# A fp32 attention and gated-scan block on Trainium2: low fp16 halves moved from GpSimd to VectorE, and the first chunk's split of x put later

## The chip, the core and the metric

The kernel runs on one NeuronCore of one Trainium2 chip. The core's engines run their own instruction queues in order: TensorE (PE; its weight loads are shown apart, as PEld), VectorE (DVE), ScalarE (ACT), GpSimd (POOL) and SyncE (SP), which here only issues DMAs. The metric is the device time of one execution in microseconds (us): the median of several runs, lower is better.

## The reference

The input x is 2 sequences of 2048 tokens with 256 features, in fp32. A layer of hierarchical linear attention comes first: 16 heads, 64 features for queries and keys, 16 for values. The weight of key s for query t is the score, times a decay that grows with the distance, times a level weight chosen by the position of s against t.

```python
decay = jnp.exp(jnp.where(tri[None, :, :, None], diff, NEG))
lam_ts = jnp.take_along_axis(Lam[:, :, :, None, :], levels[None, :, None, :, None], axis=-1)[..., 0]
scores = jnp.einsum('bthd,bshd->bhts', Q, K) * S ** (-0.5)
Wmat = scores * jnp.transpose(decay, (0, 3, 1, 2)) * jnp.transpose(lam_ts, (0, 2, 1, 3))
Y = jnp.einsum('bhts,bshd->bthd', Wmat, V).reshape(Bb, Tt, H * HD)
o = Y @ Wout.T + x
```

o is normalized, x is added, and the sum is normalized again. A gated recurrence follows. It scans over the first axis, so it has two steps, with the 2048 tokens as its batch: `c = f * c + i * g` with sigmoid and tanh gates, then `h = tanh(x @ wo.T + c_final @ uo.T + bo)`. A last residual sum and normalization give the output.

## The kernel before, in words

**Chunks.** The tokens are cut into 16 chunks of 128 (`NC`), and each chunk holds both sequences. For each chunk c the program records `load_x`, `project`, `keys`, `attend` and `finish` (the loop at the end of `body`). Within a chunk the attention is computed directly. Earlier chunks come in through states `Nst`, kept like the digits of a binary counter.

**Split numbers.** TensorE is fed fp16. An fp32 operand is split into a high half (rounded to fp16) and a low half (the fp32 value less the high half, as fp16), and a product takes three matmuls: high by high, low by high, high by low (`terms`). The halves that matter here:

- `xth`, `xtl`: x of the chunk with features on the partitions, 128x512 (`load_x`, lines 617 to 627). For chunk 0 ACT makes xth and DVE xtl. For the chunks 1 to 15 DVE casts xth and POOL subtracts to get xtl. They feed the projections `pv` (values, level weights, step sizes) and `pqk` (queries and keys).
- `xnh`, `xnl`: x with tokens on the partitions (lines 628 to 633), for the chunks 0 to 14. ACT makes xnh and POOL xnl, from the staging tile `xn`, which has one buffer.
- `wvh`, `wvl`: the decayed values `wv` (lines 751 to 756), for the chunks 0 to 14. POOL makes wv from the values and a decay `E`, ACT makes wvh, POOL wvl. The matmul `pu` multiplies xn by wv; its result becomes `Uh`, `Ul`, and through the key weights (`pS`) the chunk's state.

**Engines around them.** ACT evicts most PSUM tiles as high halves (`F` of pqk, `YT`, `Uh`, `tr_x`), takes the exponentials (`DL` of the matmul `arg`, `E`) and the gates' tanh (`tg`). DVE makes the low halves that come out of PSUM (`L`, `Ul`, `YTl`), multiplies scores by weights (`DL<-sc,DL`), and has the normalizations (`st`, `mv`, `o`, `x`, `hh`). POOL has small work on the log weights `LL` (rows of levels, decay and leaf terms), the inverse roots `rs`, `Yi`, `Yl`, the state sums and residual sums. In `project`, ACT writes logarithms into LL (two evictions from m), then cumulative sums (the eviction from `pc`). DVE splits LL into `RP`, PE transposes it, ACT evicts it as `RT`, and DMAs spread it (`cg`, `scr`, `st`, `R`) for the matmul `arg`.

**The order.** Nothing is issued while `body` runs. A `Recorder` keeps every engine call as an operation; PE calls that accumulate into one tile are joined. `depend` finds what each must wait for. `order` (lines 382 to 516) then makes one list of all operations: a list scheduler that walks through a modelled timeline and takes, for each engine, the ready operation with the earliest due time. The due times are read from the string `PLAN`, two characters per operation; the costs come from `cost`; tile buffers (`BUFS`) and PSUM banks (`BANKS`) are handed out in the same walk. `issue` (lines 518 to 529) emits the list, so that each engine's queue has its operations in that order, all of them from line 529, which is why the profile shows that line nearly everywhere. SP's queue has the DMAs in the list's order too. During the first chunk it also carries the weights: `wo` and `fw` come in 256 KB pieces through two staging buffers, ACT and DVE split them (`wo_h`, `wo_l`, `fw_h`, `fw_l`), and a piece can only be loaded when the buffer is free.

Of the kernel before, what the change touches and what calls it, by code (L numbers as in the profile page):

```python
# [110 lines left out]
    'Yh': 1, 'Yl': 1, 'acc0': 1, 'tq': 1, 'acc1': 3, 'acc2': 5, 'st69': 2, 'mv9': 10, 'rs9': 5,  # L111
}
BANKS = {'y': 8, 'z': 5, 'x': 8, 'a': 7, 's': 8, 'p': 6, 't': 5,}
MERGE, WARM, TABLE, MODE = 0.6, 0.37, 1.28, 0.1


# [36 lines left out]
class View:  # L153
# [20 lines left out]
    def real(self):  # L174
        ap = self.tile.real()
        for name, a, k in self.chain:
            ap = getattr(ap, name)(*a, **k)
        return ap
# [63 lines left out]
class Recorder:  # L242
# [139 lines left out]
    def order(self, code):  # L382
# [26 lines left out]
        for key, q in queue.items():  # L409
            free[key] = BANKS[key[1]] if key[0] == "bank" else BUFS.get(key[1], 1)  # L410
            for k, t in enumerate(q):
# [106 lines left out]
    def issue(self, plan):  # L518
        real = lambda v: v.real() if isinstance(v, View) else v
        with self.tc.manual_schedule():  # L520
            table = AF.Ln
            for i in plan:
                f = self.ops[i].fn
                if f == AF.Ln and table != f:
                    self.tc.nc.scalar.preload_act_table_set("natural_log_exp_and_others")
                if f in (AF.Ln, AF.Tanh):
                    table = f
                for eng, meth, a, k in self.ops[i].calls:
                    getattr(eng.real, meth)(*[real(x) for x in a], **{q: real(x) for q, x in k.items()})  # L529


def body(tc, A, out, nblk=NC):
    nc = tc.nc
    with ExitStack() as es:
# [2 lines left out]
        ps = es.enter_context(tc.tile_pool(name="ps", bufs=1, space=PSUM))  # L537
        dr = es.enter_context(tc.tile_pool(name="dr", bufs=1, space=DRAM))
        rec = Recorder(tc)
        V, G, ACT, PE, SP = (Engine(rec, n, e) for n, e in (  # L540
            ("DVE", nc.vector), ("POOL", nc.gpsimd), ("ACT", nc.scalar), ("PE", nc.tensor), ("SP", nc.sync)))

# [536 lines left out]
            finish(c)  # L1079
        rec.depend()  # L1080
        plan = rec.order(PLAN)
        rec.issue(plan)


# [43 lines left out]
```

## Time and profile before

| | |
|---|---|
| median of 3 runs | 613.0 us (612.38 to 614.44) |
| the profiled execution, whole | 613.06 us |
| its span, first to last instruction | 611.3 us |
| mean granted TensorE clock | 0.988 |
| DMA | 38.59 MB, 63 GB/s mean; 1 queue of SP |
| chain that ended last | PE 50%, DVE 17%, POOL 16%, ACT 8% of the span |
| largest groups of DVE | `L<-pqk,F` 85.6 us x128, `DL<-sc,DL` 84.4 us x128 |
| largest groups of POOL | `rs<-rs,mhalf` 33.8 us x45, `Yi<-Yi,tq` 24.9 us x32 |

How to read the profile: a group line has the line of code, the engine, the operation, `out<-in` by the program's names, the shape, and the count; behind the first bar the busy time in us and the mean of one in ns; behind the second the time that the engine stood idle just before them, and who ended that wait. A timeline line begins with the start and the duration in us from the span's start; idle time before it stands in brackets. A matmul's end is modelled, and matmuls overlap in the pipeline, so PE's busy time is not time at its peak. The span and the whole time differ by 1.76 us, which lie outside the first and last instruction.

### The profile page before, as it was taken

To read this page: it belongs to the slowest core of one execution; us is meant where nothing else is said; L and a number is where in the kernel's file an instruction comes from. 1 tells how busy PE (TensorE), PEld (TensorE's weight loads), DVE (VectorE), ACT (ScalarE), POOL (GpSimd) and SP (SyncE) were. 2 spreads that over 40 slices of the span, in tenths; PEclk is the share of its full clock that TensorE was granted. 3 is DMA by queue.
4 is the path that set the end of the run, shared out by engine and by line. 5 is a ranking of instruction groups with operands and counts; after the bars stand their busy time and mean duration, and the time that the engine had idled before them with its cause. 6 is when DMAs were issued, how large, how long until landed. Compare 5 with 4: busy or idle time off the path is not lost.

```text
span 611.3 us, 24225 instructions
## 1 busy us (share of the span) xinstructions
PE 578.4 (95%) x10362; PEld 499.2 (82%) x10362; DVE 495.4 (81%) x1166; ACT 395.5 (65%) x946; POOL 333.6 (55%) x677
## 2 busy tenths in 40 slices
PE   6878999999999999999999999999999999999895
PEld 3666889988898878898888988889888889888794
DVE  5678886969787986979789698896969888897985
ACT  5467687646595877568674677576577774556442
POOL 3465737334764859356593374765487663335332
PEclk9997999999999999999999999999999999999898
DMA  7753221301032103302214012130403112101101
GB/s 235 194 145 112 61 61 38 111 4 53 14 116 62 54 23 87 99 3 66 65 31 118 3 54 61 54 79 3 129 2 101 31 35 64 36 2 27 54 2 35
DMA packets 54155, 38.59 MB, mean 63 GB/s; under 512 B 16616, under 2 KB 52200, under 8 KB 54016
## 3 DMA queue, kind: packets, MB, share of 16 engines
q1 hardware_dynamic: 54048, 37.05, 21.2%
q8 instruction: 81, 1.33, 0.9%
q14 instruction: 26, 0.21, 0.1%
HBM read 29.70 MB, written 7.34 MB: 61 GB/s over the span
## 4 chain that ended last, share of the span: by engine, by line
PE 50%; DVE 17%; POOL 16%; ACT 8%; issue 4%; DMA 3%; SPq 1%; POOLq 0%; ACTq 0%; DVEq 0%
PE pqk L529 14%; PE gt L529 11%; PE sc L529 5%; PE pi L529 4%; POOL rs L529 3%; DVE st L529 2%; PE pv L529 2%; PE ph L529 2%; PE pin L529 2%; PE arg L529 2%; DMA xn<-x 2%; POOL LL L529 2%; DVE o L529 2%; PE po L529 2%; DVE DL L529 2%
## 5 line engine op out<-in xcount | busy, mean ns | idle before, releaser
L529 ACT ACTIVATE F<-pqk 128x512 f16<-128x512 f32 x128 | 75.8, 598 | 36.7 <-PE pqk L529 35.8
L529 DVE SCALAR_TENSOR_TENSOR L<-pqk,F 128x512 f16<-128x512 f32 x128 | 85.6, 679 | 12.0 <-ACT F L529 11.4
L529 PEld LDWEIGHTS <-fw_h 128*128 128x128 f16 x1176 | 91.6, 98 | 2.0 <-issue 0.2
L529 DVE SCALAR_TENSOR_TENSOR DL<-sc,DL 128x512 f32<-128x512 f32 x128 | 84.4, 680 | 7.8 <-PE sc L529 6.3
L529 PE MATMUL gt<-tr_x,fw_h 128*128 128x128 f16 x768 | 83.3, 220 | 0.9 <-DVE tr_x L529 0.8
L529 ACT ACTIVATE DL<-arg 128x512 f32<-128x512 f32 x128 | 72.4, 607 | 11.0 <-PE arg L529 10.8
L529 PEld LDWEIGHTS <-wk_h 128*128 128x128 f16 x992 | 71.0, 98 | 9.0 <-issue 2.3
L529 ACT ACTIVATE tg<-gt,gb 128x128 f32<-128x128 f32 x192 | 56.1, 372 | 34.2 <-PE gt L529 31.5
L529 PEld LDWEIGHTS <-F 64*128 64x128 f16 x2048 | 63.0, 95 | 13.1 <-issue 8.9
L529 PE MATMUL pqk<-xth,wq_h 128*128 128x256 f16 x256 | 70.2, 274 | 2.2 <-DVE Ul L529 1.9
L529 PE MATMUL gt<-tr_x,fw_l 128*128 128x128 f16 x384 | 70.3, 219 | 0.0
L529 PE MATMUL pqk<-xth,wk_h 128*128 128x256 f16 x256 | 70.2, 274 | 0.0
L529 PE MATMUL pqk<-xth,wq_l 128*128 128x256 f16 x256 | 70.1, 274 | 0.0
L529 PE MATMUL pqk<-xtl,wk_h 128*128 128x256 f16 x256 | 70.1, 274 | 0.0
L529 PE MATMUL pqk<-xtl,wq_h 128*128 128x256 f16 x256 | 70.0, 274 | 0.0
L529 PE MATMUL pqk<-xth,wk_l 128*128 128x256 f16 x256 | 70.0, 273 | 0.0
L529 PEld LDWEIGHTS <-fw_l 128*128 128x128 f16 x588 | 57.4, 98 | 1.7 <-issue 1.0
L529 PEld LDWEIGHTS <-wq_h 128*128 128x128 f16 x512 | 47.1, 98 | 10.8 <-issue 3.7
L529 PE MATMUL sc<-F 64*128 64x128 f16 x512 | 48.6, 222 | 2.1 <-ACT F L529 1.6
L529 PEld LDWEIGHTS <-wk_l 128*128 128x128 f16 x496 | 46.3, 98 | 4.3 <-issue 1.0
L529 PE MATMUL arg<-R,st 96*128 96x64 f16 x1024 | 45.3, 193 | 3.6 <-ACT DL L529 2.1
L529 PE MATMUL sc<-F,L 64*128 64x128 f16 x512 | 47.6, 221 | 0.5 <-DVE L L529 0.5
(185 smaller groups left out, 1842.2 us busy)
## 6 DMA issues: line engine op xcount, KB each, us to landing
st<-cg SPq DMA_DIRECT2D x16, 512.0 KB
xt<-xT SPq DMA_DIRECT2D x16, 256.0 KB
xc<-x SPq DMA_DIRECT2D x16, 256.0 KB
xn<-x SPq DMA_DIRECT2D x15, 256.0 KB
out<-hh SPq DMA_DIRECT2D x15, 256.0 KB
scr<-RT SPq DMA_DIRECT2D x16, 160.0 KB
R<-scr SPq DMA_DIRECT2D x32, 80.0 KB
stg_fw<-fw SPq DMA_DIRECT2D x8, 256.0 KB
```

What stands on the lines that cost most here:

```text
L529: getattr(eng.real, meth)(*[real(x) for x in a], **{q: real(x) for q, x in k.items()})
```

## The change

It does two things after the plan is made; `PLAN`, `BUFS`, costs and the recorded operations are as they were, so `order` returns the same list as before.

First, at issue, every operation whose result is xtl, xnl or wvl, and which was recorded for POOL, is emitted on DVE instead, at its place in the list. Second, three operations are moved within the list: ACT's first xnh goes behind the last operation of chunk 0 that ACT does into LL (the eviction of pc), the first xnl behind the last operation of chunk 0 that POOL does into E, and the load of xn for chunk 1 behind that xnl, since xn has one buffer.

```diff
+LOW = ("POOL:xtl", "POOL:xnl", "POOL:wvl")
...
                 for eng, meth, a, k in self.ops[i].calls:
+                    if self.ops[i].kind.split("@")[0] in LOW:
+                        eng = self.dve
                     getattr(eng.real, meth)(*[real(x) for x in a], **{q: real(x) for q, x in k.items()})
...
         rec = Recorder(tc)
+        rec.dve = Engine(rec, "DVE", nc.vector)
...
         plan = rec.order(PLAN)
+
+        seen = lambda kind: [k for k, i in enumerate(plan) if rec.ops[i].kind == kind]
+        for kind, other in (("ACT:xnh@0", "ACT:LL@0"), ("POOL:xnl@0", "POOL:E@0"), ("DMA:xn", "POOL:xnl@0")):
+            a, b = seen(kind)[0], seen(other)[-1]
+            if a < b:
+                plan.insert(b, plan.pop(a))
         rec.issue(plan)
```

## The prediction

> **What bounds the kernel now.** I read, in this order: the busy shares and slices, a table by stretches, the groups by form, and the timelines of ACT, DVE and POOL at the places of the change. The page's shares and slices first (tenths of each fortieth of the span; PEclk is the granted TensorE clock):
>
> ```profile
> PE 578.4 (95%) x10362; PEld 499.2 (82%) x10362; DVE 495.4 (81%) x1166; ACT 395.5 (65%) x946; POOL 333.6 (55%) x677
> ...
> PE   6878999999999999999999999999999999999895
> ...
> PEclk9997999999999999999999999999999999999898
> ```
>
> PE is full from slice 5 on; DVE comes second. The table by stretches (stretch, its length, then busy us of PE, PEld, DVE, ACT, POOL, the granted clock, DMA):
>
> ```profile
> 20.00:60.00 40.00, 31.29 (x400) 24.46 (x398) 28.39 (x51) 25.57 (x60) 23.50 (x52) 0.92 0.52 149
> 60.00:150.00 90.00, 89.47 (x1758) 78.13 (x1757) 74.17 (x176) 60.89 (x145) 44.80 (x88) 1.00 0.20 57
> 150.00:300.00 150.00, 147.37 (x2708) 127.72 (x2706) 125.49 (x300) 104.58 (x255) 91.55 (x189) 1.00 0.21 60
> 300.00:450.00 150.00, 146.10 (x2621) 127.21 (x2618) 123.32 (x284) 101.83 (x246) 87.95 (x184) 1.00 0.19 54
> 450.00:570.00 120.00, 116.80 (x2187) 101.81 (x2180) 101.02 (x254) 73.94 (x178) 67.24 (x128) 1.00 0.15 42
> ```
>
> From 20 to 60 us PE is idle 40.00 − 31.29 = 8.7 us, at a clock below 1. From 60 to 570 us it is idle only 510 − 499.7 = 10.3 us. There DVE is busy 424.0 of 510 us, so idle 86. A gain can come from the first 60 us; a loss comes where DVE hands PE its next operand late. DVE has spare time on the mean; whether it has it where the new instructions stand decides.
>
> **The change, part by part.**
>
> *What moves.* I compared the two programs engine by engine. PE's order is the same. POOL loses 45 instructions and DVE gains them (15 each of xtl, xnl, wvl), at the place of the common order where they stood. On ACT the first xnh goes from ahead of the two LL evictions of m to just behind the LL eviction of pc. On SP one 256 KB load of fw goes ahead of the xn load of chunk 1. The rows that price the 45:
>
> ```profile
> L529 POOL TENSOR_TENSOR xtl<-xt,xth 128x512 f16<-128x512 f32 x15 | 18.3, 1223 | 11.3 <-DVE xth L529 11.3
> L529 POOL TENSOR_TENSOR xnl<-xn,xnh 128x512 f16<-128x512 f32 x15 | 18.1, 1207 | 30.3 <-ACT xnh L529 30.3
> L529 POOL TENSOR_TENSOR wvl<-wv,wvh 128x512 f16<-128x512 f32 x15 | 18.1, 1205 | 3.0 <-ACT wvh L529 3.0
> ```
> ```profile
> L529 DVE TENSOR_TENSOR xtl<-xt,xth 128x512 f16<-128x512 f32 x1 | 0.7, 693 | 1.8 <-ACT xth L529 1.8
> ```
>
> The last row is the same operation on DVE, seen once: 0.69 us. In a row of like instructions DVE starts the next 0.60 to 0.61 us later (two L of 0.68 take 1.29 in its timeline), so each new one costs the queue behind it 0.61 us: 45 × 0.61 = 27.5 us of DVE, against 54.5 us taken off POOL.
>
> *What comes back.* A large POOL instruction holds some DVE instructions up:
>
> ```profile
> 35.76 1.54 DVE L529 SCALAR_TENSOR_TENSOR m<-z 128x416 f32<-128x416 f32 x1
> ```
> ```profile
> 35.70 1.15 POOL L529 TENSOR_TENSOR xtl<-xt,xth 128x512 f16<-128x512 f32 x1
> ```
>
> m<-z takes 0.58 us elsewhere; here it lasts to the end of POOL's xtl and 0.4 beyond. Over the trace I summed, for DVE instructions that lay beside one of the 45, the time above the tenth percentile of their form: 8.6 us in 15 places. So DVE's net gain in load is 27.5 − 8.6 = 18.9 us. [...]
>
> *First chunk (20 to 57 us).* ACT now:
>
> ```profile
> 25.01 0.63 ACT L529 ACTIVATE xnh<-xn 128x512 f16<-128x512 f32 x1 [4.66 <-DMA xn<-x]
> 25.54 0.32 ACT L529 ACTIVATE LL<-m 128x160 f32<-128x160 f32 x1
> ...
> 27.27 0.64 ACT L529 ACTIVATE wo_h<-stg_wo 128x512 f16<-128x512 f32 x1
> ...
> 28.26 0.65 ACT L529 ACTIVATE fw_h<-stg_fw 128x512 f16<-128x512 f32 x1
> 28.78 0.24 ACT L529 ACTIVATE LL<-pc 128x64 f32<-128x64 f32 x1
> ```
>
> ACT stands 4.66 us before xn, whose last part lands at 24.98 by the trace's completions. Behind it wait two LL, three F, VZ and all the weight splits. PE loses 1.62 us at 24.8 and 0.49 at 26.6 to those F and to their L: 2.1 us that go. But not 4.66 us: ACT then reaches wo_h, whose load lands only at 26.92, so wo_h starts 27.27 − 26.95 = 0.3 us earlier than now, LL<-pc ends at 28.7 instead of 29.02, and behind it now stands xnh (0.52). What is late next: POOL's E no longer waits behind its leaf work (30.92 now); it goes to 28.8. wv, wvh and RT follow; RT's end, 34.61 now, goes to about 32.4 (E<-E 29.7, two Ne to 30.15, wv 31.2, wvh 31.9, RT 32.4): 2.2 us. On DVE the new xnl stands ahead of RP and waits for xnh, to 29.3, then 0.69: RP starts at 30.1 instead of 31.00, a gain of 0.9 there. wvl, now on DVE, ends at 33.2 instead of 35.24, and pu with it: 2.0 us. The second chunk's xnl waits 0.34 us on DVE for its xnh, with u<-m,u, an Ul and L behind it; with the four new instructions between 35 and 54 us that is 0.34 + 4 × 0.61 = 2.8 us, and the held-up m (twice), fw_l and u give 0.96 + 0.96 + 0.97 + 0.37 = 3.3 back, so I set it at nothing. The moved xn load now waits for xnl (30.1 instead of 26.9), with a load of fw behind it at 30.5 instead of 29.9; xn is not read before about 36, so nothing. I take **−2.0 us** for this part; the ends are 0 (the L and DMA waits around 40 to 50 us eat it) and −5.4. The lower end has 3.4 us for the clock: it is granted at half from 53.9 to 60.75 us, with PE busy throughout, so 6.83 × 0.5 = 3.4 us hang on PE's idle time just before (0.67, 0.28 and 1.04 us at 49.4 to 52.2, for L and for ACT's DL).
>
> *After 60 us.* The semaphores tell which DVE instruction each PE instruction waits for. For every new place I followed them from the DVE instruction behind it and took the least time that lies free before some PE instruction would start late. Delay is 0.61 per new instruction, plus its wait, less DVE's idle time there, less what collisions give back. In us:
>
> 61.6 xnl: 0.59 wait + 0.61, free 0.07: loss 1.1. 102.8 to 115.5, three: 1.83, free 0.91: 0.9. 175 to 179, two: 1.22, free 0.37: 0.85. 210 to 216, three: 1.83 − 0.75 given back, free 0.03: 1.05. 286 to 288, three: 1.83 − 0.34, free 0.35: 1.1. 318 to 329, four: 2.44 − 1.60, free 0.67: 0.2. 393 to 405, three: 1.83 − 0.77, 0.36 idle: 0.7. 429 to 432, three: 1.83 − 0.31, free 0.05: 1.5. 463 to 471, three: 1.83 − 0.71, free 0.12: 1.0. The other 13 together 0.8, eight of them nothing (76, 90, 188, 230, 241, 362, 485, 494: free 0.9 to 3.3, or as much idle or given back).
>
> Sum 9.2 us; with the 2.7 above the upper end is 11.9. The lower end is 0: DVE's 86 us of idle time, and 1.9 us that PE waits for POOL (gp at 206 and 354, Yl at 411 and 456) which POOL, relieved of a sixth of its work, may give back. The places were priced one by one, and PE, once late, is late for the next one too, so they add up to less than 9.2. I take the middle, **+6.0 us**.
>
> *Sum.* 611.3 − 2.0 + 6.0 = 615.3 us of span. The profiled execution took 613.06 us, 1.76 us around its span; it is level with the median of 613.0. So **617.0 us**.
>
> **Rivals.** (a) *Hidden*, 612: the new instructions fall into DVE's idle time and only the first chunk's −2.0 and about +1 remain. For it: 86 us of idle. Against it: from 102 to 125 and from 319 to 339 us DVE's idle time adds up to under 0.7 us, against 1.8 and 2.4 us of new instructions. (b) *Faster*, 609: the half-clock stretch at 53.9 us goes. PE's idle time of 2.0 us at 49.4 to 52.2 us would have to shrink, which it does if ACT has wvh and DL out earlier; 613.06 − 2.0 − 3.4 + 1.4 = 609.1. It decides the sign from a loss under 5.4 us after 60 us. [...] (c) *DVE the bound*, 630: each of the 45 is charged in full, 613.06 + 18.9 − 2.0; for it, DVE at 81% would be at (495.4 + 18.9)/611 = 84%; against it, 97 us of idle would remain on the mean. (d) *Level*, 613 to 614.8: first chunk and rest cancel.
>
> **Numbers.** A measurement of this kernel tells 0.3% from no change, 1.8 us. Forecast (615 to 622) 0.47, (a) 0.20, half of it below 611.2, (b) 0.12, of which 0.10 below 611.2, (c) 0.11, (d) 0.10. Faster 0.10 + 0.10 = 0.20; same 0.10 + 0.02 + 0.10 = 0.22; slower 0.58. The range takes in (b), at 609.0, and reaches to 613.06 + 11.9 = 625.0, which leaves out (c) and a little else. The forecast's own range is 615 to 622.
>
> **What would show it.** First chunk: ACT's wait of 4.66 us before xnh gone, its idle time now before wo_h, RT ending near 32.4 us, PE idle in 20:60 at 6.7 instead of 8.7. After: PE's idle in 60:570 up from 10.3 to about 16, ended by DVE (Ul, L, DL, tr_x); DVE busy near 514; m<-z back at 0.58. It would be wrong if PE's idle after 60 us stays near 10, or if xnl is found waiting for xnh on DVE for more than the 0.3 to 0.6 us worked out here.

## The result, and the profile after

The changed kernel takes 619.85 us (median of 4 runs, 619.0 to 620.99), the kernel before 612.95 us beside it: ratio 1.0109, 95% interval 1.0096 to 1.0122, so it is slower by 1.1%. The profiled execution took 620.22 us, its span is 618.4 us (before 611.3), the mean clock 0.988 as before.

The page after, the lines that answer to those of before:

```profile
PE 581.0 (94%) x10362; PEld 499.9 (81%) x10362; DVE 513.0 (83%) x1211; ACT 395.8 (64%) x946; POOL 285.8 (46%) x632
...
PE   5797999999999999999999999999999999999895
...
PEclk9997999999999999999999999999999999999899
```

DVE has its 45 instructions more (1211 against 1166) and is 17.6 us busier; POOL is 47.8 us less busy. The table by stretches, same columns as before:

```profile
20.00:60.00 40.00, 32.73 (x436) 25.11 (x434) 31.74 (x60) 25.87 (x60) 16.21 (x45) 0.88 0.53 152
60.00:150.00 90.00, 88.32 (x1726) 77.18 (x1719) 75.02 (x180) 59.86 (x145) 37.37 (x81) 1.00 0.19 56
150.00:300.00 150.00, 145.20 (x2636) 124.92 (x2634) 129.80 (x306) 101.70 (x249) 74.70 (x172) 1.00 0.22 60
300.00:450.00 150.00, 144.79 (x2546) 125.61 (x2544) 126.80 (x298) 100.14 (x238) 74.70 (x162) 1.00 0.20 54
450.00:570.00 120.00, 118.44 (x2185) 103.39 (x2182) 100.11 (x244) 77.86 (x188) 60.35 (x128) 1.00 0.13 37
```

PE's idle time is 7.3 us from 20 to 60 (before 8.7) and 510 − 496.75 = 13.25 us from 60 to 570 (before 10.3). That is not the whole loss: for the matmuls that stand from 60 to 570 us in the trace of before, PE's busy time grows from 499.7 to 502.9 us, though they are the same matmuls, so part of the loss is counted as busy. A better measure is the start of each matmul. Both kernels have the same 10362 in the same order, so the traces can be laid side by side, matmul by matmul. PE is ahead of before by 1.02 us at 43 us and by 1.48 at 57 us; it is behind by 0.47 at 150, 4.2 at 300, 6.0 at 450 and 6.9 at 560 us. This "lag" is used from here on; it compares one execution with one.

The 1.48 at 57 us is not all gain. In both traces the clock is at half rate for 6.83 us, from 53.92 us before and from 54.00 after. The lead is 1.02 us up to that stretch, and since the same work reaches the stretch 1 us earlier, more of it runs ahead of the stretch at the full rate; at the other end this goes back, and the lead is 1.10 us where PE meets the first wait after it:

```profile
62.12 1.08 PE L532 MATMUL pi<-DL,VZ 128*32 128x128 f32 x32 [0.82 <-DVE DL L532]
```

So the first chunk gave 1.0 us, and what follows took 7.9.

The moved subtractions, by form, on DVE:

```profile
L532 DVE TENSOR_TENSOR xtl<-xt,xth 128x512 f16<-128x512 f32 x16 | 11.8, 738 | 1.9 <-ACT xth L532 1.9
L532 DVE TENSOR_TENSOR wvl<-wv,wvh 128x512 f16<-128x512 f32 x15 | 10.8, 723 | 0.7 <-ACT wvh L532 0.7
...
L532 DVE TENSOR_TENSOR xnl<-xn,xnh 128x512 f16<-128x512 f32 x15 | 10.3, 687 | 0.7 <-ACT xnh L532 0.7
```

They take 0.69 to 0.74 us. The xnl wait 0.7 us in all and the wvl 0.7 us; the 1.9 us before xtl belong to chunk 0, whose xtl was on DVE before too. The m that was held up takes 0.59 us again:

```profile
35.04 0.59 DVE L532 SCALAR_TENSOR_TENSOR m<-z 128x416 f32<-128x416 f32 x1
```

**One place in detail.** How the time is lost shows where three of the 45 stand close together. DVE's timeline before (start, duration), then after:

```profile
428.69 0.73 DVE L529 TENSOR_SCALAR hh<-hh,mv,rs 128x256 f32<-128x256 f32 x2
429.35 0.68 DVE L529 SCALAR_TENSOR_TENSOR L<-pqk,F 128x512 f16<-128x512 f32 x1
...
431.38 0.67 DVE L529 SCALAR_TENSOR_TENSOR DL<-sc,DL 128x512 f32<-128x512 f32 x1
...
432.31 0.67 DVE L529 TENSOR_TENSOR Ul<-pu,Uh 128x512 f16<-128x512 f32 x1
```
```profile
433.24 0.74 DVE L532 TENSOR_SCALAR hh<-hh,mv,rs 128x256 f32<-128x256 f32 x2
433.89 0.69 DVE L532 TENSOR_TENSOR xtl<-xt,xth 128x512 f16<-128x512 f32 x1
434.49 0.69 DVE L532 SCALAR_TENSOR_TENSOR L<-pqk,F 128x512 f16<-128x512 f32 x1
...
436.22 0.68 DVE L532 TENSOR_TENSOR xnl<-xn,xnh 128x512 f16<-128x512 f32 x1
436.81 0.69 DVE L532 SCALAR_TENSOR_TENSOR DL<-sc,DL 128x512 f32<-128x512 f32 x1
...
437.74 0.68 DVE L532 TENSOR_TENSOR wvl<-wv,wvh 128x512 f16<-128x512 f32 x1
438.33 0.69 DVE L532 TENSOR_TENSOR Ul<-pu,Uh 128x512 f16<-128x512 f32 x1
```

DVE comes here 4.55 us late (hh). L is 5.14 us later than before, DL 5.43, Ul 6.02: DVE has no pause, so each new instruction adds its 0.6 us, less 0.3 that the two `o<-o,rs,xc` take without POOL's subtraction beside them (0.88 us instead of 1.18). PE, also 4.5 us late when it comes here, stands twice and leaves 6.0 us late:

```profile
437.55 0.27 PE L532 MATMUL pqk<-xth,wq_h 128*128 128x256 f16 x1 [0.32 <-DVE DL L532]
439.08 0.40 PE L532 MATMUL arg<-R,st 96*128 96x64 f16 x8 [0.71 <-DVE Ul L532]
```

The waits shown are single short ones (the longest after 60 us is 1.05 us); no line of the page holds the loss. Nor does POOL's relief come through: its wait for DVE's m ahead of g is 42.0 us instead of 16.0, for DVE's z 48.4 instead of 32.7. And POOL's own work grew longer: 54.5 us of instructions went, its busy time fell by 47.8 only.

**The first chunk.** ACT no longer waits for xn; it waits for wo's load instead:

```profile
26.73 0.63 ACT L532 ACTIVATE wo_h<-stg_wo 128x512 f16<-128x512 f32 x1 [3.62 <-DMA stg_wo<-wo]
27.26 0.58 ACT L532 ACTIVATE F<-pqk 128x512 f16<-128x512 f32 x1
27.74 0.62 ACT L532 ACTIVATE fw_h<-stg_fw 128x512 f16<-128x512 f32 x1
28.26 0.21 ACT L532 ACTIVATE LL<-pc 128x64 f32<-128x64 f32 x1
```

LL<-pc stands behind it, RP on DVE behind LL, xnl and two weight splits. PE's two stops of 1.62 and 0.49 us (for F and L) are gone and it runs 2.9 us ahead, to stand 3.46 us in one piece. The first two rows are from the kernel after, the third from the kernel before:

```profile
30.79 0.71 PE L532 MATMUL pt<-idh,RP 128*128 128x128 f16 x5 [3.46 <-DVE RP L532]
...
41.79 0.36 PE L532 MATMUL pv<-wv_h,xth 128*128 128x464 f16 x1 [0.63 <-DVE L L532]
```
```profile
42.82 0.36 PE L529 MATMUL pv<-wv_h,xth 128*128 128x464 f16 x1 [0.80 <-DVE L L529]
```

The last two rows are the same matmul, the last common point: PE waits there for an L of DVE before and after, and leaves 1.02 us earlier.

### The profile page after: what moved, and what is told of

It reads as the page before. It is cut to its first block, busy times and chain, and to the rows that moved or that the text cites. A ratio compares the mean times of both kernels' runs of the same rounds, so it can differ in the third digit from the quotient of the medians.

```text
span 618.4 us, 24210 instructions
## 1 busy us (share of the span) xinstructions
PE 581.0 (94%) x10362; PEld 499.9 (81%) x10362; DVE 513.0 (83%) x1211; ACT 395.8 (64%) x946; POOL 285.8 (46%) x632
## 4 chain that ended last, share of the span: by engine, by line
PE 44%; DVE 27%; POOL 12%; ACT 7%; issue 5%; DMA 4%; SPq 1%; POOLq 0%; ACTq 0%; DVEq 0%
PE gt L532 12%; PE pqk L532 8%; PE sc L532 4%; DVE L L532 4%; PE pi L532 4%; POOL rs L532 3%; DVE st L532 3%; DVE DL L532 3%; PE pv L532 3%; DVE o L532 2%; PE ph L532 2%; PE pin L532 2%; DMA xn<-x 2%; PE po L532 2%; PE arg L532 2%
## 5 line engine op out<-in xcount | busy, mean ns | idle before, releaser
L532 ACT ACTIVATE tg<-gt,gb 128x128 f32<-128x128 f32 x192 | 56.1, 371 | 35.4 <-PE gt L532 32.7
L532 PEld LDWEIGHTS <-L 64*128 64x128 f16 x1024 | 47.0, 95 | 1.7 <-issue 1.1
```

## The experiments

Times are medians; the ratio is to the kernel before on the same chip, with its 95% interval. The last four columns are PE's lag against before, in us (negative: ahead), at that time of the trace of before; each is of one execution, and the executions of one kernel lie 1 to 4.4 us apart. Lags at 57 us lie inside the half-rate stretch that every kernel has there and are distorted by it. The two kernels with copies leave the low halves concerned out, so they are no versions to use.

| kernel | us | ratio | 43 | 57 | 150 | 560 |
|---|---|---|---|---|---|---|
| the change | 619.85 | 1.0109 [1.0096, 1.0122] | −1.0 | −1.5 | +0.5 | +6.9 |
| moves only | 611.63 | 0.9986 [0.9971, 1.0000] | −1.0 | −0.9 | 0.0 | −0.3 |
| halves only | 620.47 | 1.0131 [1.0114, 1.0148] | −1.2 | −0.7 | +1.2 | +7.8 |
| moves, 16 free halves | 611.19 | 0.9975 [0.9965, 0.9985] | −1.2 | −1.2 | −1.9 | −1.9 |
| moves, 29 costly halves | 620.23 | 1.0135 [1.0118, 1.0152] | −0.7 | −1.2 | +1.5 | +8.1 |
| both engines subtract | 645.54 | 1.0537 [1.0507, 1.0567] | +1.8 | +2.1 | +6.7 | +32.5 |
| copies in place of halves | 609.12 | 0.9946 [0.9924, 0.9967] | −2.8 | −3.4 | −2.9 | −4.9 |
| change, RP ahead | 620.72 | 1.0136 [1.0097, 1.0174] | −1.1 | −0.7 | +2.6 | +9.2 |
| 16 free, RP ahead | 610.88 | 0.9970 [0.9953, 0.9987] | −1.2 | −1.7 | −2.2 | −2.0 |
| and 2 fw splits late | 611.83 | 0.9963 [0.9942, 0.9984] | −1.7 | −1.9 | −2.6 | −2.1 |
| and 4 fw splits late | 616.23 | 1.0033 [1.0018, 1.0048] | −4.2 | +2.6 | +2.3 | +2.9 |
| change, PE kept busy | 619.93 | 1.0087 [1.0062, 1.0113] | −1.7 | −1.5 | +0.5 | +7.0 |
| change, 5 early copies | 619.14 | 1.0072 [1.0049, 1.0095] | −2.3 | −2.0 | 0.0 | +6.5 |

**Where the loss comes from.** Theory A: each added instruction makes DVE's operands late by its own length, at the places without free time, and these add. The rivals: the moves of the first chunk cost it (B), or DVE's load as such does, wherever the instructions stand (C). The first four kernels split the change in two ways: by its two parts, and by the places that the prediction had priced at nothing or nearly so (16) and the rest (29).

```diff
-LOW = ("POOL:xtl", "POOL:xnl", "POOL:wvl")
+LOW = ()
```

> The three moves in the list alone; all low halves stay on POOL. Theory A (late operands: an instruction put on DVE costs where PE's next operand from DVE has less free time than the 0.61 us it takes, and these losses add up): nothing changes after 60 us, the first chunk gains 0.5 to 2 us, so 611.0 to 612.5 us. Rival B (the moves in the list are what costs): 615 us or more, PE 3 us or more later than before at 60 us.

For the second, the five lines after `rec.order(PLAN)` that move three operations are left out.

> The 45 low halves on DVE, the list's order as before. Theory A: the loss of 8 us after 60 us stays, the first chunk gains nothing (DVE now waits for xn as ACT does), so 620 to 623 us. Rival B (the moves in the list cost): 613 us or less.

For the third and fourth, LOW lists which of the 15 of each kind go to DVE:

```diff
+LOW = {"xtl": (1, 2, 3, 11), "xnl": (1, 2, 4, 8, 15), "wvl": (1, 2, 3, 6, 8, 11, 15)}
...
-                    if self.ops[i].kind.split("@")[0] in LOW:
+                    if nth[low] in LOW.get(low, ()):
```

> As the change, but of the 45 only the 16 that the prediction priced at about nothing are on DVE (seven in the first 60 us, nine later), 29 stay on POOL. Theory A: level with the moves alone to within 1 us, 611 to 613 us. Rival C (DVE's added load counts wherever it stands): 16/45 of the 8 us on top of the moves alone, 614.5 us.

> As the change, but only the other 29 on DVE, in the places that the prediction priced (and four that it priced at 0.1 to 0.3 us). Theory A: nearly all of the loss after 60 us, 7 to 8 us above the moves alone, 618.5 to 620.5 us. Rival C (load wherever it stands): 29/45 of 8 us, 5.2 us above the moves alone, 617 us.

The moves alone are level (611.63). The halves alone have the whole loss (620.47), and the gain of the first chunk as well (1.2 us at 43 us), which the expectation had at nothing. The 16 free ones cost nothing: 611.19 against 611.63 for the moves alone, with intervals that overlap, so a gain is not shown. The 29 have the whole loss again, 8.1 us at 560 us. B and C fall. The parts add: at 560 us, 16 free and 29 costly stand 1.6 under and 8.4 above the moves alone; −0.3 − 1.6 + 8.4 = 6.5, and the change has 6.9.

**DVE's own time, or its consumers?** In one kernel POOL keeps its 45 and DVE does each a second time into a spare tile; in another DVE has a copy of the high half at each place instead of the subtraction, so that the low half is left out.

```diff
-                        eng = self.dve
+                        self.dve.real.tensor_tensor(self.spare, real(a[1]), real(a[2]), a[3])
```

> The 45 subtractions stay on GpSimd, as before the change, and the vector engine does each of them a second time, into a tile that nobody reads, at the place where the changed kernel has it; the moves of the first chunk are in. (Nothing of the computation is left out; the second copies are extra work.) Theory A (the vector engine's own later operations come late, by the 0.6 to 0.75 us that each added instruction occupies, at places where little is free): the same loss as the change, 619 to 623 us, more than the change rather than less, because GpSimd now works beside it. Rival (the time is lost because TensorE, the consumer, waits for halves that now come late out of the vector engine's queue): consumers get their halves from GpSimd as before, so 611 to 613 us.

```diff
-                        eng = self.dve
+                        self.dve.real.tensor_copy(real(a[0]), real(a[2]))
+                        continue
```

> The changed kernel, with each of the 45 subtractions on the vector engine replaced by a copy of the high half (fp16 to fp16), which I estimate at 0.2 to 0.4 us from the vector engine's CAST 128x512 (0.42 us) against 0.69 to 0.74; the low halves are then wrong, this part of the computation is left out. Theory A (loss is the time that the added instruction occupies at places with little free time, beyond the first part that is free): most of the loss goes, 612 to 615 us. Rival (the loss is a matter of order and waits: the vector engine's queue stands until ScalarE has made the high half, whatever the length of the instruction): 618 to 620 us.

Both decide for A, and both missed in size. The useless second subtraction costs 32.5 us, nearly five times the change, although nobody reads it. Its rows, by form:

```profile
L531 DVE TENSOR_TENSOR spare<-xt,xth 128x512 f16<-128x512 f32 x15 | 18.2, 1214 | 0.0
L531 DVE TENSOR_TENSOR spare<-xn,xnh 128x512 f16<-128x512 f32 x15 | 15.1, 1004 | 0.7 <-ACT xnh L532 0.7
L531 DVE TENSOR_TENSOR spare<-wv,wvh 128x512 f16<-128x512 f32 x15 | 15.0, 1000 | 1.7 <-ACT wvh L532 1.7
```

Both engines become ready at the same moment and read the same two tiles: DVE takes 1.00 to 1.21 us instead of 0.69, POOL 1.29 to 1.42 instead of 1.21 to 1.22. That is 48 us of DVE instead of 31. POOL's halves come later too, but that is not what PE waits for. Over the matmuls that stand between 60 and 570 us in the trace of before, PE's waits that end on DVE sum to 5.4 us before, 10.6 in the change, 26.2 here and 4.0 with the copies; those that end on POOL stay at 1.9, 1.7, 2.0 and 1.7. The copies (median 0.28 us, mean 0.28 to 0.34) take nearly the same places and the loss is gone, with 4.9 us gained at 560 us. So what counts at these places is the length of the new instruction, not that one stands there. Where the 4.9 us come from was not separated.

**Why the first chunk gave less.** First theory (part of Theory A in the next two expectations, B' later): the one standstill of 3.46 us ahead of RP, and the half-rate window that follows it, are what is missing. Two kernels put the splits of wo, of the first fw and of xn, and gb, behind RP, once in the changed kernel, once with the 16 free halves:

```diff
+        a, b = seen("ACT:wo_h@0")[0], seen("DVE:RP@0")[-1]
+        names = ("ACT:wo_h@0", "DVE:gb@0", "DVE:wo_l@0", "ACT:fw_h@0", "DVE:fw_l@0", "DMA:stg_fw@0",
+                 "ACT:xnh@0", "POOL:xnl@0")
+        late = [i for i in plan[a:b] if rec.ops[i].kind in names]
+        plan[a:b + 1] = [i for i in plan[a:b + 1] if i not in late] + late
         rec.issue(plan)
```

> The changed kernel, with one more move in the first chunk: the operations that split the loads of wo and of the first fw, gb and the first chunk's x (two of them wait for loads that land at 26.2 and 26.7 us) are placed behind the second RP, so that the LL <- pc of ScalarE and the two RP of the vector engine don't queue behind them. Theory A (of the gain in the first chunk, the part that is missing sits in the one standstill of TensorE ahead of RP, 3.46 us from 27.3 to 30.8, and in the half-rate window that follows it, some 1.7 us): the standstill shrinks to below 1 us, and 2.5 to 5 us come off, 615 to 617.5 us. Rival (the next wait, the transposed RT with its way through the scratch in DRAM or the weights' splits, takes its place): 619 to 620.5 us.

> The same move on top of the version with the 16 halves that cost nothing on the vector engine and the other 29 on GpSimd (611.2 us, where the standstill ahead of RP is 3.81 us with no half-rate window behind it). Theory A: 2 to 3.5 us off, 607.5 to 609.5 us, faster than both kernels. Rival (another wait takes its place): 610.5 to 611.5 us.

The standstill goes, and nothing is gained: 620.72 and 610.88. PE stands elsewhere, and goes on at 41.7 us, where it waits for the L, as in the changed kernel. PE's rows in the changed kernel with RP ahead, then the row of ACT that is behind the second:

```profile
30.61 0.27 PE L532 MATMUL pqk<-xth,wq_h 128*128 128x256 f16 x1 [2.03 <-DVE L L532]
37.42 0.27 PE L532 MATMUL pqk<-xth,wq_h 128*128 128x256 f16 x1 [2.72 <-DVE Ul L532]
```
```profile
34.61 0.63 ACT L532 ACTIVATE fw_h<-stg_fw 128x512 f16<-128x512 f32 x1 [3.60 <-DMA stg_fw<-fw]
```

So two theories were left. C (the letter is used anew from here on): DVE's row of work up to that L sets the end (in the changed kernel the timeline shows 0.3 us of idle time between 27.4 and 42.3 us). D: the landing of fw's pieces does. Two kernels put the next two fw splits behind Ul, or those behind the third L after it and the following two behind five DL:

```diff
+        def late(names, a, b):
+            moved = [i for i in plan[a:b] if rec.ops[i].kind in names]
+            plan[a:b + 1] = [i for i in plan[a:b + 1] if i not in moved] + moved
...
+        fw = ("ACT:fw_h@0", "DVE:fw_l@0", "DMA:stg_fw@0")
+        late(fw, seen("ACT:fw_h@0")[1], seen("DVE:Ul@0")[-1])
```

> The version with 16 halves on the vector engine and the move ahead of RP (610.9 us), in which the split of the second and third load of fw (fw_h on ScalarE, fw_l on the vector engine) is also placed behind the first chunk's second Ul. Theory C (the end of the first chunk is set by the vector engine, which has hardly a pause from 27.4 us to the L that TensorE awaits at 41.7; a step that only changes the order ahead of that L gives nothing): TensorE is at 42.8 us where it was, 610 to 611.5 us. Theory D (it is set by the landing of the fw load, for which ScalarE stood 3.6 us ahead of 34.6 us once RP came early): the 2 us that TensorE stood ahead of Ul go, 607.5 to 609.5 us.

```diff
-        late(fw, seen("ACT:fw_h@0")[1], seen("DVE:Ul@0")[-1])
+        late(fw, seen("ACT:fw_h@0")[1], [k for k in seen("DVE:L") if k > seen("DVE:Ul@0")[-1]][2])
+        late(fw, seen("ACT:fw_h@0")[3], seen("ACT:DL@0")[4])
```

> As the run before, but the splits of the second and third load of fw are placed behind the third L that follows Ul, and the next two behind the first five DL of ScalarE. Theory C: two fw_l (0.69 us each) leave the vector engine's row ahead of the L at 41.7, so TensorE is 1.0 to 1.4 us ahead from 42.8 us on, 608.5 to 610 us, unless pg, which needs the fifth fw_l, then waits (it would by 1 us or more: 610 to 611). Theory D: no further gain over the run before.

With the first of them PE's wait for the first Ul goes (2.0 us with 16 free halves and RP ahead), and its wait for L doubles from 0.6 to 1.2 us. PE gains 0.5 us at 43 us, not 2, and none of it is left at 560 us: D falls as a bound of 2 us. The moved fw_l still stand ahead of that L. With the second, two fw_l no longer do, and PE is 4.2 us ahead at 43 us. It reaches the matmul behind that L 3.0 us earlier than with RP ahead alone: 0.8 because wo landed earlier in that execution, 1.2 because two fw_l left DVE's row, and 1.0 because DVE stands less in that row, which had 0.9 us of waiting for the load of fw. So C holds for the 1.2, and D has a share of about 0.9. Then pg pays for it, which needs the fifth fw_l:

```profile
57.88 0.18 PE L535 MATMUL pg<-ich,fw_l 128*128 128x1 f16 x1 [4.34 <-DVE fw_l L535]
```

That wait of 4.34 us was more than the 1 us that the expectation allowed, the clock stays at half for 17 us, and the kernel takes 616.23 us.

Two more kernels test the half-rate window and DVE's row apart. One fills the standstill with transposes that nobody needs, the other has copies for the five halves between 20 and 42 us:

```diff
+                    if self.ops[i].kind == "PE:pt@0" and not self.warm:
+                        self.warm = 28
+                        for _ in range(self.warm):
+                            eng.real.transpose(real(a[0]), real(a[2]), real(a[2]))
```

> The changed kernel, with 28 more transposes (of the identity, into the place that RP's transposes overwrite) ahead of the first chunk's RP transposes, so that TensorE works for some 2.5 of the 3.46 us from 27.3 to 30.8 in which it stood. Extra work only. Expected by both: no half-rate window at 30.1 us. Theory B' (that window is what the first chunk's gain lacks): 1 to 1.7 us off, 618 to 619 us. Theory C (the vector engine's L at 41.8 us is waited for anyway): TensorE is ahead from 31 to 39 us and no longer at 42.8; 619.5 to 620.5 us.

```diff
+SHORT = {"POOL:xtl": 2, "POOL:xnl": 2, "POOL:wvl": 1}
...
                         eng = self.dve
+                        if nth[low] <= SHORT[low]:
+                            eng.real.tensor_copy(real(a[0]), real(a[2]))
+                            continue
```

> The changed kernel, with five of the 45 subtractions (xtl and xnl of the first two of their places, wvl of the first: those from 20 to 42 us) replaced by the copy of the high half, 0.28 us instead of 0.69 (those low halves are wrong, that part of the computation is left out). Theory C: four of them lie in the vector engine's unbroken row from 27.4 to 41.8 us, 4 x 0.41 = 1.6 us; TensorE is 1.4 to 1.9 us further ahead at 42.8 us, and 618 to 618.6 us result (TensorE's 0.8 us wait for DL at 62 takes none of it). Theory B' (the half-rate window at 30.1 sets it): no change at 42.8 us as long as that window stays, 619.5 to 620.5 us.

With the transposes the half-rate window at 30.1 us is gone, and PE is 0.7 us further ahead at 43 us, 0.3 of it because wo landed earlier. But PE starts pi at 62.12 us in both, where it waits for a DL of DVE (0.54 us instead of 0.82), and the half-rate stretch ahead of it lasts 10.24 us instead of 6.83. From there on the lags are the same: nothing lasts, and B' falls. With the copies PE is 2.3 us ahead at 43 us, 1.3 more than the change. But wo landed 0.7 us earlier in that execution, so part of it is not the copies. From the start of wo_l to the matmul that waits for the L, it is 14.4 us in the changed kernel, 14.0 with the transposes, 13.9 with the five copies and a half-rate window at 30 us, 12.8 with copies and no such window (the kernel with 45 copies), and 12.1 with two fw_l out of the row. DVE stands for 0.5 us of the 14.4 and 0.2 of the 14.0, short gaps included, so its row sets nearly all of it; by these single executions the window takes 0.4 us where DVE has the long instructions and 1.0 us where it has the short ones. Of the copies' 1.3 us, 0.5 are left at 66 us, behind a half-rate stretch that lasts 10.2 us instead of 6.8. The time, 619.14 us, lies between what the two theories expected.

A version faster than both kernels: the moves with the 16 free halves, 611.19 us, ratio 0.9975. RP ahead (0.9970) and two fw splits late (0.9963) cannot be told from it. The gain is 0.25 to 0.4%, the size of what can be measured.

## Why the prediction was right or wrong

The direction was right, on the mechanism it named: DVE hands operands over late at places without free time. The time, 619.85 us, is inside its own range of 615 to 622 and 2.9 us above the forecast of 617.0. Two terms of the sum were mis-sized, both to the same side: +6.0 after 60 us, which measured +7.9, and −2.0 in the first chunk, which measured −1.0.

- **Terms that held.** DVE's busy time is 513.0 us ("near 514"). m<-z is back at 0.59 us beside xtl's old place. What collisions take from DVE, summed as in the prediction but over all of POOL's instructions, fell from 25.0 to 16.8 us: 8.2 against the 8.6 worked out for the 45. No run shows the 2.7 us in the upper end of the sum; the moved subtractions themselves lose about 1.2 us (32.9 us busy for 46 of 0.69). The wait for xn is gone and wo_h is the next wait, as written; RP starts at 29.89 (30.1 worked out).
- **The larger error: the discount after 60 us.** The list of places summed to 9.2 us; the prediction then said that "they add up to less than 9.2" and took 6.0, the middle. They did add up to less, but only to 7.9. By the lag, the nine named places cost 0.9 (predicted 1.1; the half-rate stretch's share taken off), 0.6 (0.9), 1.0 (0.85), 1.1 (1.05), 1.3 (1.1), −0.3 (0.2), 0.4 (0.7), 1.5 (1.5) and 1.0 us (1.0), 7.5 against 8.4. Two places of the others, at 142 to 152 and 246 to 254 us, cost 0.7 and 0.6, which makes 8.8; 0.9 was given back between the places, 0.65 of it from 72 to 80 us. The reason given for the discount, that PE once late is late for the next place too, leaves out that DVE can be late along with it. At 429 us it is: both come 4.5 us late, so DVE's distance to PE is the old one and the place costs its full 1.5 us. That this holds at every place was not followed up; that the kernels with 16 and 29 of the halves add fits it.
- **The first chunk, −2.0, was −1.0.** The sum took the 2.0 us of pu and the 2.2 us of RT as the way to the gain. Both came later than worked out. RT was to end at 32.4 us and wvl at 33.2; both only start then and end at 33.11 and 33.88, so they gain 1.5 and 1.4 us. One reason is on POOL, where Nt and the two Ne ahead of wv take 1.87 us instead of 1.00, beside fw_l, xnl and RP on DVE, so that the second Ne ends at 30.84 instead of the 30.15 worked out. Before, then after:

```profile
31.25 0.31 POOL L529 TENSOR_SCALAR Nt<-LL 128x32 f32<-128x32 f32 x1
31.65 0.69 POOL L529 TENSOR_SCALAR Ne<-E 64x16 f32<-64x16 f32 x2
```
```profile
28.89 0.62 POOL L532 TENSOR_SCALAR Nt<-LL 128x32 f32<-128x32 f32 x1
29.59 1.25 POOL L532 TENSOR_SCALAR Ne<-E 64x16 f32<-64x16 f32 x2
...
30.81 1.05 POOL L532 TENSOR_TENSOR wv<-VZ,E 128x512 f32<-128x512 f32 x1
```

  And PE then waits not for pu or RT but for DVE's row up to the L at 41.05 us, which gained 1.04 us, about what the prediction had for RP alone (0.9; measured 1.15). Behind RP two things hold that row, side by side. One is ich, which now meets POOL's wv; both end together. The other is z, which waits for VZ of ACT and through it for PE's pv, which runs in the half-rate window at 30.1 us and ends at 33.74. The first row is from before, the others from after:

```profile
31.80 0.17 DVE L529 CAST ich<-ic 128x2 f16<-128x2 f32 x1
```
```profile
30.65 1.24 DVE L532 CAST ich<-ic 128x2 f16<-128x2 f32 x1
...
34.19 0.38 DVE L532 TENSOR_TENSOR z<-pv,LpB 128x208 f32<-128x208 f32 x1 [0.31 <-ACT VZ L532]
```

  Since z waits, a short ich alone would not have let it start earlier; and where the window is gone (the transposes), z does not wait, ich still takes 1.24 us, and 0.4 us are gained. With RP ahead both are gone, and the load of fw takes over. From z (0.72 us ahead) to the L the row gained 0.3, so "I set it at nothing", which was said of DVE there, was about right. Each part of the change alone gives this much too (−1.0 moves, −1.2 halves): they end at the same L, and they do not add.
- **The rivals.** Hidden (612) falls with PE's waits above; it is right for 16 of the 45. The vanished half-rate stretch (609) did not come: it lies at 54.0 us for 6.83 us, as before. That it hangs on PE's idle time just ahead was the prediction's estimate and is not shown for this stretch: in the 3.4 us ahead of the stretch PE is idle for 1.62 us before and 1.27 after. Fully charged (630): no, DVE's pauses do take up part: 18.9 us of net load cost 7.9. Level: no, 1.0 us of gain does not stand against 7.9.
- **PE's idle time** in 60:570 was to rise to 16 and rose to 13.25, with a larger loss. The measure was a poor one: part of the loss is counted as busy.

## What to carry to other kernels

Work moved to an engine that feeds the bound engine is priced place by place: the length of the new instruction, less the free time at that place. The places then add up to nearly their sum (7.9 of 9.2 us here): where it was looked at, the engine that comes late had fallen back together with the one it feeds. The spare time on the mean (19% of DVE here) says nothing about them; the same 45 moves held 16 that cost nothing and 29 that had the whole loss. What is taken off an engine may not all be saved there: POOL's remaining instructions took 6.7 us longer. Where one wait is taken away from a start-up stage with several queues, look for the chain that all variants meet next (here DVE's row up to one L): a wait that goes ahead of it only moves.

## What the runs showed of the hardware

- **The half clock came in stretches of 3.41 us or a multiple.** In the kernel before and in the changed one the half-rate stretches that end within the work last 3.41 and 6.83 us; with the transposes and with the 5 early copies one lasts 10.24, with 4 fw splits late one lasts 17.07 us. Within each of the first two executions the starts are whole multiples apart: in the changed kernel 30.11, 54.00 and 579.66 us, 7 and 154 times 3.413 apart, in the kernel before 53.93 and 572.75 us, 152 times. In the changed kernel PE's standstill of 3.46 us (27.32 to 30.78) fills 82% of the 3.41 us ahead of the first of these, 26.70 to 30.11. In the kernel with 16 free halves a longer one, 3.81 us from 27.22, has none behind it (the granted clock is 1.00 from 27 to 50 us); counted back in steps of 3.413 us from that execution's next half-rate stretch, it falls across two steps, of which PE is busy 47% and 41%. What share of idle time brings on the half clock the runs do not settle: each kernel has a stretch that begins between 48 and 55 us, behind 3.41 us of which PE was busy 33 to 64%, and in two kernels a half-rate stretch comes behind 3.41 us of which PE was busy 73% (the 29 costly halves, at 217.9 us) and 83% (both engines subtract, at 351.8 us), while the two steps of 47% and 41% had none behind them.
- **Taking a half-rate window away gained nothing here.** Without the one at 30.1 us the kernel is no faster (619.93 against 619.85 us, 1.0087 [1.0062, 1.0113] against 1.0109 [1.0096, 1.0122]). PE was 0.4 us earlier for it at the L, but the half-rate stretch that followed was 3.41 us longer (10.24 against 6.83), and PE met the same wait for DVE at 62.12 us.
- **A tiny instruction took as long as a large one.** The cast of 128x2 takes 0.16 to 0.17 us in nine of the kernels, and 1.24 us in the five where POOL's wv (1.05 us) starts 0.16 us behind it. In the changed kernel the cast starts first in the profile, at 30.65 us against 30.81, yet ends 0.03 us after wv. What holds it that long was not shown.
